# Neighbour sums of steps 2 and 3: one float32 matmul, or two float32r matmuls on a split operand

## The chip, the core and the metric

The kernel runs on one core of one Trainium2 chip. The metric is device microseconds (us) for one execution of the whole program. A core has a matrix engine (TensorE, PE in the profile; its weight loads have a row of their own, PEld), a vector engine (VectorE, DVE), a scalar engine (ScalarE, ACT), GpSimd (POOL), and SyncE (SP), which here only starts transfers. TensorE writes its results to PSUM; the other engines must copy them from there to SBUF before TensorE can use them again as an operand.

## What is computed

There are 128 graphs of 128 nodes with 256 features, and an integer adjacency matrix for each. Layer 0 is a gated graph network of three steps, followed by a residual and a layer norm; layers 1 to 3 are graph attention layers, each with a residual and a layer norm. The part that the change touches is the neighbour sum of layer 0:

```python
A = (adj != 0).astype(x.dtype)
h = x
for i in range(3):
    m = jnp.einsum('bnd,de->bne', h, weight[i])
    aggr = jnp.einsum('bst,bsd->btd', A, m)
    h = _gru_cell(aggr, h, w_ih, w_hh, b_ih, b_hh)
x = _layernorm(x + h)
# then three attention layers with the same adj, e.g.
# Wh = h @ W.T; e = leaky(a1.Wh_i + a2.Wh_j), masked by adj; softmax; h' = att @ Wh
# x = _layernorm(x + h')
```

The kernel sums the neighbours first and multiplies by the weights afterwards (the step's weight and the input weight of the cell are multiplied together once, at the start), so a neighbour sum is a product of h, as it stands, with the 0-or-1 mask A.

## The kernel before

Four graphs make a group (`G = 4`), so the 128 graphs are 32 groups. A group goes through three steps of the gated network (`gru`) and three attention layers (`gat`). All of it is float32.

One step of `gru` does this for a group, for each of the two halves `c` of the 256 features:

1. Line 504: the neighbour sum. For each of the four graphs one matmul takes a 128x128 piece of h (nodes on the partitions) as the stationary operand and the 128x128 mask `am` as the moving operand. The four results fill one PSUM tile called `bank`. Line 506 copies (evicts) it to SBUF, on ScalarE (line 287) or VectorE (line 289), as the planner chooses.
2. Line 421 (`sums`): sums of halves for a Strassen-like scheme, on GpSimd or VectorE.
3. Line 451: the gate matmuls, with 128x128 weights (`whs` for the hidden state, `wcs` for the neighbour sum) and 256 moving columns, and line 456, which adds partial results out of PSUM on VectorE.
4. Lines 530 to 569: the sigmoids (as tanh), the tanh, and the new state, as `hT2`, with features on the partitions.
5. Line 585: the new state is transposed on TensorE back to nodes on the partitions, into a `bank`; line 593 evicts it as `h2`, which is the h of the next step's line 504. After the last step there is no `h2`; the state is added to x instead.

In step 1, h is the input x itself (`xs`), so only the line 504 of steps 2 and 3 uses `h2`. Its matmuls have the names `bank<-am,k` in the profile; those of step 1 have `bank<-am,xs`.

PSUM is split into 5 tiles called `gate` and 3 called `bank`. In SBUF, `k2` names 26 tiles of 512 floats, `k4` 19 of 1024.

The order of work is a plan made when the program is built. `Plan.op` records each piece of work with a cost in ns for every engine that may do it; `Plan.order` runs an event-driven list schedule over these costs, with the older group first, tiles handed out as they come free, and a number of tiles (`own`) kept back for the oldest group. The result fixes the order of the instructions of every engine and, where there is a choice, the engine. Several groups are in work at once, so while one group waits for a vector operation, TensorE works on another group's gates. The costs are only used to plan; on the chip each engine takes its instructions in that order and waits on semaphores.

Of the kernel before, what the change touches and what calls it, by code (L numbers as in the profile page):

```python
# [7 lines left out]

F32 = mybir.dt.float32
I32 = mybir.dt.int32  # L10
AF = mybir.ActivationFunctionType
ALU = mybir.AluOpType
AX = mybir.AxisListType

P = 128
D = 256
KC = D // P
G = 4
# [5 lines left out]
FAR = -5.0 * 2.0 ** 97  # L24
# [174 lines left out]
def adj_resnorm_kernel(  # L199
# [14 lines left out]
    nc = tc.nc  # L214
# [5 lines left out]
    work = ctx.enter_context(tc.tile_pool(name="work", bufs=1))  # L220
# [2 lines left out]

    pools = {"gru": 4, "xs": 2, "adj": 2, "am": 5, "k2": 26, "k4": 19, "fx": 2, "f": 3, "mv": 4, "st": 6, "v": 16,
             "gate": 5, "bank": 3}
    own = ({"k2": 8, "k4": 5, "gate": 2, "v": 5, "fx": 0, "st": 0}, {"k2": 4, "k4": 2, "v": 5, "fx": 0, "st": 0})
    floats = {"gru": 0, "k4": 1024, "xs": 1024, "fx": 256, "f": 8, "mv": 8, "st": 6, "v": 4}
    tags = {t: (n, floats.get(t, 512)) for t, n in pools.items()}
    BOTH = ("DVE", "POOL")
    plan = Plan({t: n for t, (n, _) in tags.items()}, own)  # L230
    slots = {t: [(psum if t in ("gate", "bank") else work).tile([P, w], I32 if t == "adj" else F32, name=f"{t}{i}")
                 for i in range(n)] for t, (n, w) in tags.items() if w}

    def T(b):
        if b.at is None:
            width = 1
            for s in b.shape:
                width *= s
            at = slots[b.tag][b.slot][:, 0:width]
            if len(b.shape) == 2:  # L240
                at = at.rearrange("p (a b) -> p a b", b=b.shape[-1])
            elif len(b.shape) == 3:
                at = at.rearrange("p (a b c) -> p a b c", b=b.shape[-2], c=b.shape[-1])
            b.at = at
        return b.at

    def bank():
        return Buf("bank", GN)

    def here(t):  # L250
        b = Buf(None)
        b.at = t
        return b


    ident = consts.tile([P, P], F32)
    make_identity(nc, ident)
# [3 lines left out]
    A11, A12, N22, S1, S2, S3, S4 = range(7)  # L261
    whs = here(consts.tile([P, 7, 3, P], F32, name="whs"))

    wcs = [here(consts.tile([P, 7, 3, P], F32, name=f"wcs{i}")) for i in range(STEPS)]
    gwT = here(consts.tile([P, 3, KC, D], F32, name="gwT"))
    wa = here(consts.tile([P, 3, 2, D], F32, name="wa"))
    bi = consts.tile([P, 3 * KC], F32, name="bi")
# [17 lines left out]
    def copy(e, dst, src):  # L285
        if e == "ACT":
            nc.scalar.copy(dst, src)  # L287
        else:
            nc.vector.tensor_copy(dst, src)  # L289

    LAND = 1500
    EVICT = {"ACT": 490, "DVE": 600}
    EVICT2 = {"ACT": 370, "DVE": 350}

    def load(dst, src, prio, start=0):

        plan.op({"SP": 450}, lambda e: nc.sync.dma_start(T(dst), src), writes=[dst], prio=prio, lag=LAND, start=start)
# [16 lines left out]
    def hidden_weights(prio):  # L314
        raw = [Buf("k4", 3 * D) for k in range(KC)]
        for k in range(KC):
            load(raw[k], w_hhT[:, k], prio)
        for k in range(KC):

            plan.op({"DVE": 430}, lambda e, k=k: nc.vector.tensor_scalar(  # L320
                T(raw[k])[:, 2 * D:3 * D], T(raw[k])[:, 2 * D:3 * D], 0.5, None, op0=ALU.mult),
                reads=[raw[k]], writes=[raw[k]], prio=prio)
        block_sums(whs, lambda c, k: T(raw[k]).rearrange("p (g c d) -> p g c d", g=3, c=KC)[:, :, c, :], [[r] for r in raw], prio)
# [153 lines left out]
    def gru(g, stage):  # L477

        xs, adj_i, am = Buf("xs", G, D), Buf("adj", G, P), Buf("am", G, P)
        prio = stage(g, 0)  # L480
# [4 lines left out]
                writes=[adj_i], prio=prio)  # L485
        if g == 0:
            input_weights(0, prio)
            hidden_weights(prio)
        plan.op({"DVE": 417}, lambda e: nc.vector.tensor_scalar(T(am), T(adj_i), 0, None, op0=ALU.not_equal),
                reads=[adj_i], writes=[am, turn], prio=prio, port=BOTH)  # L490
        hT = transposed(xs, lambda b, c: T(xs)[:, b, c * P:(c + 1) * P], prio)
        h = None
        for i in range(STEPS):
            prio = stage(g, i)
# [3 lines left out]
            for c in range(KC):  # L498
                b_, a_ = bank(), Buf("k2", GN)

                def fn(e, b_=b_, c=c, h=h):
                    for b in range(G):
                        src = T(xs)[:, b, c * P:(c + 1) * P] if h is None else T(h[c])[:, b, :]
                        nc.tensor.matmul(T(b_)[:, b * P:(b + 1) * P], src, T(am)[:, b, :], start=True, stop=True)  # L504
                plan.op({"PE": 4 * 222}, fn, reads=[am, xs if h is None else h[c]], writes=[b_], prio=prio)
                plan.op(EVICT, lambda e, b_=b_, a_=a_: copy(e, T(a_), T(b_)), reads=[b_], writes=[a_], prio=prio)
                agg.append(a_)
            last = i == STEPS - 1
# [16 lines left out]
            for c in range(KC):  # L525

                o, v, d = rz[c], nn[c], Buf("k2", GN)
# [4 lines left out]
                for gt in range(2):  # L532
                    if c == 0:
                        plan.op({"ACT": 630}, lambda e, gt=gt, o=o, tanh=tanh: tanh(gt, 0, GN, lambda: T(o)[:, gt, :]),
                                reads=[(o, 0), (o, 1)], writes=[(o, 2 + gt)], prio=prio)
                    else:
                        plan.op({"ACT": 365}, lambda e, gt=gt, tanh=tanh, rz=rz: tanh(
                            gt, 0, H, lambda: T(rz[2])[:, gt * H:(gt + 1) * H]),
                            reads=[rz[2]], writes=[(o, 4 + gt)], prio=prio)
                        plan.op({"ACT": 400}, lambda e, gt=gt, o=o, tanh=tanh: tanh(gt, H, GN, lambda: T(o)[:, gt, H:GN]),  # L540
                                reads=[(o, 1), (o, 4 + gt)], writes=[(o, 2 + gt)], prio=prio)
                if c == 1:
                    plan.op({"ACT": 370}, lambda e, v=v, nn=nn: nc.scalar.activation(
                        T(v)[:, 0, 0:H], T(nn[2])[:, 0:H], AF.Identity, bias=bhn[:, 1:2]),
                        reads=[nn[2]], writes=[(v, 0)], prio=prio)
                plan.op({"DVE": 620}, lambda e, o=o, v=v: nc.vector.scalar_tensor_tensor(
                    T(v)[:, 0, :], T(o)[:, 0, :], 1.0, T(v)[:, 0, :], op0=ALU.add, op1=ALU.mult),
                    reads=[(o, 2), (v, 0), (v, 1)], writes=[(v, 2)], prio=prio, port=BOTH)
                if c == 0:
                    plan.op({"DVE": 620}, lambda e, v=v: nc.vector.tensor_add(T(v)[:, 0, :], T(v)[:, 1, :], T(v)[:, 0, :]),  # L550
                            reads=[(v, 2)], writes=[(v, 3)], prio=prio, port=BOTH)
                else:
                    plan.op({"DVE": 350}, lambda e, v=v, nn=nn: nc.vector.tensor_add(
                        T(v)[:, 0, 0:H], T(nn[2])[:, H:GN], T(v)[:, 0, 0:H]),
                        reads=[(v, 2), nn[2]], writes=[(v, 3)], prio=prio)
                    plan.op({"DVE": 350}, lambda e, v=v: nc.vector.tensor_add(  # L556
                        T(v)[:, 0, H:GN], T(v)[:, 1, H:GN], T(v)[:, 0, H:GN]),
                        reads=[(v, 2)], writes=[(v, 4)], prio=prio, port=BOTH)
                plan.op({"ACT": 630}, lambda e, v=v, c=c: nc.scalar.activation(  # L559
                    T(v)[:, 0, :], T(v)[:, 0, :], AF.Tanh, bias=bin_[:, c:c + 1]),  # L560
                    reads=[(v, 3), (v, 4)], writes=[(v, 5)], prio=prio)
# [3 lines left out]
                    reads=[hT[c], (v, 5)], writes=[d], prio=prio, port=BOTH)  # L565
                plan.op({"DVE": 620}, lambda e, d=d, o=o: nc.vector.scalar_tensor_tensor(
                    T(d), T(o)[:, 1, :], 1.0, T(d), op0=ALU.add, op1=ALU.mult),
                    reads=[(o, 3), d], writes=[d], prio=prio, port=BOTH)
                plan.op({"DVE": 620}, lambda e, d=d, v=v: nc.vector.scalar_tensor_tensor(  # L569
                    T(d), T(d), 0.5, T(v)[:, 0, :], op0=ALU.mult, op1=ALU.add),  # L570
                    reads=[d, (v, 5)], writes=[d], prio=prio, port=BOTH)
                hT2.append(d)
            if last:
                y = Buf("k4", G, D)
                plan.op({"SP": 60}, lambda e: nc.sync.dma_start(T(y), x_g), reads=[agg[0]], writes=[y], prio=prio)
                plan.op({"DVE": 417}, lambda e: nc.vector.tensor_scalar(
                    T(am), T(am), 0.0, FAR, op0=ALU.is_equal, op1=ALU.mult), reads=[am], writes=[am], prio=prio, port=BOTH)
            else:
                h2 = [Buf("k2", G, P) for c in range(KC)]
            for c in range(KC):  # L580
                b_ = bank()

                def fn(e, b_=b_, c=c, hT2=hT2):
                    for b in range(G):
                        nc.tensor.transpose(T(b_)[:, b * P:(b + 1) * P], T(hT2[c])[:, b * P:(b + 1) * P], ident)  # L585
                plan.op({"PE": 440}, fn, reads=[hT2[c]], writes=[b_], prio=prio)
                if last:
                    plan.op({"DVE": 620}, lambda e, b_=b_, c=c, y=y: nc.vector.tensor_add(
                        T(y)[:, :, c * P:(c + 1) * P], T(b_).rearrange("p (b d) -> p b d", b=G),
                        T(y)[:, :, c * P:(c + 1) * P]), reads=[b_, turn, (y, 0)],  # L590
                        writes=[(y, b) for b in range(G)], prio=prio)
                else:
                    plan.op(EVICT, lambda e, b_=b_, c=c, h2=h2: copy(
                        e, T(h2[c]), T(b_).rearrange("p (b d) -> p b d", b=G)), reads=[b_], writes=[h2[c]], prio=prio)
            if not last:
                h, hT = h2, hT2
        x1 = Buf("k4", G, D)
# [98 lines left out]
    def stage(g, n):  # L696

        tail = NG - LAST
        return g if g < tail else tail + n, 2 * g + (n >= STEPS)

    for g in range(NG):
        gat(g, *gru(g, stage), stage)
# [47 lines left out]
```

## Time and profile before

| | before |
|---|---|
| time, median of 3 runs (range) | 2700.24 us (2698.6 to 2702.52) |
| span in the profile, granted TensorE clock | 2698.8 us, 0.998 |
| neighbour sums of steps 2 and 3: TensorE instructions | 1024 weight loads and 1024 matmuls (L504, `bank<-am,k`) |
| evictions of `bank` tiles to `k` tiles (all, not only of `h2`) | 456 on ScalarE, mean 583 ns; 228 on VectorE, mean 684 ns |

A page of the profile gives, for each group of equal instructions, the source line, engine and operation, the names of output and inputs, the shape, how many there were, the busy time and the mean duration of one, and then how long the engine stood idle just before them and what ended that. Busy times of TensorE overlap, because matmuls are pipelined; the step from one start to the next says more than the duration. The chain of waits is followed back from the last instruction and says which engine's work set the end.

A float32 matmul of the source stands in the trace as two weight loads and two matmuls; a transpose stands as one of each.

### The profile page before, as it was taken

To read this page: it belongs to the slowest core of one execution; us is meant where nothing else is said; L and a number is where in the kernel's file an instruction comes from. 1 tells how busy PE (TensorE), PEld (TensorE's weight loads), DVE (VectorE), ACT (ScalarE), POOL (GpSimd) and SP (SyncE) were. 2 spreads that over 40 slices of the span, in tenths; PEclk is the share of its full clock that TensorE was granted. 3 is DMA by queue.
4 is the path that set the end of the run, shared out by engine and by line. 5 is a ranking of instruction groups with operands and counts; after the bars stand their busy time and mean duration, and the time that the engine had idled before them with its cause. 6 is when DMAs were issued, how large, how long until landed. Compare 5 with 4: busy or idle time off the path is not lost.

```text
span 2698.8 us, 42460 instructions
## 1 busy us (share of the span) xinstructions
PE 2655.6 (98%) x14536; PEld 2366.9 (88%) x14536; DVE 2019.6 (75%) x6195; ACT 1758.2 (65%) x4633; POOL 603.7 (22%) x749
## 2 busy tenths in 40 slices
PE   8999999999999999999999999999999999999997
PEld 7888889898888888888888888988988988888875
DVE  4676777787777787778777777877778776786796
ACT  4565667666667576666666676666666676765478
POOL 1123222222121221222221221211222211322111
PEclk9999999999999999999999999999999999999999
DMA  3100000000000000001010000000000100000000
GB/s 106 32 13 28 28 13 24 28 29 20 16 21 20 28 28 28 28 1 36 21 36 13 20 24 21 28 28 20 17 28 21 36 21 1 24 9 22 19 1 32
DMA packets 70105, 65.39 MB, mean 24 GB/s; under 512 B 2688, under 2 KB 68224, under 8 KB 69888
## 3 DMA queue, kind: packets, MB, share of 16 engines
q1 hardware_dynamic: 69456, 62.66, 7.7%
q8 instruction: 114, 1.87, 0.3%
q14 instruction: 103, 0.84, 0.1%
q10 hardware_dynamic: 432, 0.01, 0.0%
HBM read 45.89 MB, written 16.78 MB: 23 GB/s over the span
## 4 chain that ended last, share of the span: by engine, by line
PE 90%; DVE 6%; ACT 2%; issue 1%; DMA 0%; POOL 0%; POOLq 0%; ACTq 0%; SPq 0%; DVEq 0%
PE gate L451 61%; PE bank L680 10%; PE bank L504 6%; PE bank L669 6%; PE bank L585 3%; PE bank L620 1%; PE bank L653 1%; DVE fx L611 1%; PE bank L369 1%; PE bank L338 1%; DVE k L686 1%; ACT k L407 1%; DVE k L456 1%; DVE k L289 1%; ACT k L394 0%
## 5 line engine op out<-in xcount | busy, mean ns | idle before, releaser
L451 PE MATMUL gate<-k,whs 128*128 128x256 f32 x4032 | 1201.6, 380 | 3.0 <-DVE k L456 1.4
L451 PE MATMUL gate<-k,wcs 128*128 128x256 f32 x4032 | 1199.2, 379 | 0.0
L451 PEld LDWEIGHTS gate<-k,wcs 128*128 128x128 f32 x4032 | 766.1, 190 | 104.0
L451 PEld LDWEIGHTS gate<-k,whs 128*128 128x128 f32 x4032 | 728.5, 190 | 85.3 <-DVE k L456 2.7
L456 DVE TENSOR_TENSOR k<-gate,k 128x512 f32<-128x512 f32 x576 | 390.4, 686 | 242.3 <-PE gate L451 200.2
L287 ACT COPY k<-bank 128x512 f32<-128x512 f32 (+1 forms) x456 | 262.2, 583 | 207.4 <-PE bank L669 60.9
L680 PE MATMUL bank<-gwT,k 128*128 128x256 f32 x1536 | 350.4, 380 | 3.3 <-ACT k L287 1.5
L680 PEld LDWEIGHTS bank<-gwT,k 128*128 128x128 f32 x1536 | 289.7, 190 | 46.0 <-DVE k L289 4.3
L611 DVE SCALAR_TENSOR_TENSOR fx<-k,wa 128x256 f32<-128x256 f32 x768 | 290.3, 436 | 40.3 <-ACT k L407 38.2
L421 POOL TENSOR_TENSOR k<-k,k 128x256 f32<-128x256 f32 x288 | 236.0, 838 | 372.8 <-DVE k L569 103.6
L394 ACT ACTIVATE k<-k,v 128x256 f32<-128x256 f32 x384 | 190.2, 497 | 185.6 <-DVE v L391 185.1
L407 ACT ACTIVATE k<-k,v,v 128x256 f32<-128x256 f32 x512 | 263.6, 591 | 55.9 <-DVE v L403 53.9
L530 ACT ACTIVATE k<-k,brz 128x512 f32<-128x512 f32 (+1 forms) x384 | 226.9, 620 | 93.2 <-DVE k L456 93.1
L686 DVE SCALAR_TENSOR_TENSOR k<-bank,v,k 128x256 f32<-128x256 f32 x384 | 169.9, 480 | 147.0 <-PE bank L680 145.8
L512 ACT COPY k<-gate 128x512 f32<-128x512 f32 x288 | 164.6, 579 | 127.9 <-PE gate L451 127.0
L564 POOL TENSOR_TENSOR k<-k,k 128x512 f32<-128x512 f32 x82 | 108.5, 1324 | 418.0 <-ACT k L559 418.0
L669 PEld LDWEIGHTS bank<-k,k 128*128 128x128 f32 x1536 | 187.1, 193 | 14.6 <-ACT k L287 5.4
L669 PE MATMUL bank<-k,k 128*128 128x128 f32 x1536 | 189.8, 277 | 8.0 <-DVE k L289 4.0
L289 DVE COPY k<-bank 128x512 f32<-128x512 f32 x228 | 154.3, 684 | 56.2 <-PE bank L504 18.3
L559 ACT ACTIVATE k<-k,bi 128x512 f32<-128x512 f32 x192 | 136.8, 720 | 76.3 <-DVE k L556 59.2
L397 POOL TENSOR_SCALAR v<-v 128x4 f32<-128x4 f32 x96 | 21.1, 220 | 739.3 <-ACT k L394 733.3
L421 POOL TENSOR_TENSOR k<-k 128x256 f32<-128x256 f32 x117 | 100.2, 858 | 340.4 <-DVE k L569 118.2
(78 smaller groups left out, 3166.8 us busy)
## 6 DMA issues: line engine op xcount, KB each, us to landing
xs<-in_x_dram SPq DMA_DIRECT2D x32, 512.0 KB, 3.9
k<-in_x_dram SPq DMA_DIRECT2D x32, 512.0 KB, 3.9
out_dram<-k SPq DMA_DIRECT2D x32, 512.0 KB, 2.9
adj<-in_adj_dram SPq DMA_DIRECT2D x32, 256.0 KB, 2.8
k<-in_gnn_wT_dram SPq DMA_DIRECT2D x3, 256.0 KB, 4.8
k<-in_w_ihT_dram SPq DMA_DIRECT2D x2, 384.0 KB, 5.7
k<-in_w_hhT_dram SPq DMA_DIRECT2D x2, 384.0 KB, 5.7
k<-in_gat_w_dram SPq DMA_DIRECT2D x3, 256.0 KB, 5.1
```

What stands on the lines that cost most here:

```text
L287: nc.scalar.copy(dst, src)
L289: nc.vector.tensor_copy(dst, src)
L394: plan.op({"ACT": 490}, lambda e, b=b: nc.scalar.activation(T(dst)[:, b, :], T(y)[:, b, :], AF.Square, bias=T(mean)[:, b:b + 1], accum_out ...
L407: plan.op({"ACT": 500}, lambda e, b=b: nc.scalar.activation(T(dst)[:, b, :], T(y)[:, b, :], AF.Identity, bias=T(shift)[:, b:b + 1], scale= ...
L421: nc.vector if e == "DVE" else nc.gpsimd).tensor_tensor(T(t)[:, j, :], a(), b(), ALU.subtract),
L451: nc.tensor.matmul(T(dst)[:, j * H:(j + 1) * H], T(w)[:, m, gt, :], moving(m, ms)[1](), start=first and n == 0, stop=n == len(todo) - 1, s ...
L456: plan.op({"DVE": 630}, lambda e: nc.vector.tensor_add(T(o)[:, :, j * H:(j + 1) * H], T(b_).rearrange("p (g n) -> p g n", g=2), T(part).re ...
L530: nc.scalar.activation(T(o)[:, gt, n0:n1], src(), AF.Tanh, bias=brz[:, gt * KC + c:gt * KC + c + 1], scale=0.5)
L611: plan.op({"DVE": 345}, lambda e, b=b, h=h, l=l, f=f, fx=fx, xc=xc: nc.vector.scalar_tensor_tensor(T(fx), T(xc)[:, b, :], 1.0, T(wa)[:, l, ...
L669: nc.tensor.matmul(T(b_)[:, b * P:(b + 1) * P], T(xc)[:, b, c * P:(c + 1) * P], T(pT)[:, b, :], start=True, stop=True)
L680: nc.tensor.matmul(T(b_)[:, (b - b0) * D:(b - b0 + 1) * D], T(aT[k])[:, b * P:(b + 1) * P], T(gwT)[:, l, k, :], start=(k == 0), stop=(k == ...
L686: nc.vector.scalar_tensor_tensor(T(y)[:, b, :], T(b_)[:, (b - b0) * D:(b - b0 + 1) * D], T(rden)[:, b:b + 1], T(xc)[:, b, :], op0=ALU.mult ...
```

## The change

The neighbour sum of steps 2 and 3 is done in float32r, a form of float32 with a shorter mantissa. The mask is 0 or 1 and therefore exact in it. h is split: `hi` is h rounded to float32r as it is evicted, `lo` is the rest, h minus `hi`, also stored as float32r. Two float32r matmuls then add `lo` and `hi` products into the same PSUM tile. The purpose is to replace the two-load, two-matmul float32 product by a form that needs fewer passes through TensorE, at the price of one more vector operation for `lo`.

```diff
-    own = ({"k2": 8, "k4": 5, ...
+    own = ({"k2": 10, "k4": 5, ...
...
+    FRESH = ("k2", "am")
...
+            if b.tag in FRESH:
+                at = work.tile([P, tags[b.tag][1]], F32, tag=f"{b.tag}{b.slot}", name=b.tag)[:, 0:width]
+            else:
+                at = slots[b.tag][b.slot][:, 0:width]
...
+    def R(b):
+        return T(b).bitcast(F32R)
...
-        plan.op({"DVE": 417}, lambda e: nc.vector.tensor_scalar(T(am), T(adj_i), 0, None, op0=ALU.not_equal),
+        plan.op({"DVE": 417}, lambda e: nc.vector.tensor_scalar(R(am), T(adj_i), 0, None, op0=ALU.not_equal),
...
-                        src = T(xs)[:, b, c * P:(c + 1) * P] if h is None else T(h[c])[:, b, :]
-                        nc.tensor.matmul(T(b_)[:, b * P:(b + 1) * P], src, T(am)[:, b, :], start=True, stop=True)
-                plan.op({"PE": 4 * 222}, fn, reads=[am, xs if h is None else h[c]], writes=[b_], prio=prio)
+                        dst = T(b_)[:, b * P:(b + 1) * P]
+                        if h is None:
+                            nc.tensor.matmul(dst, T(xs)[:, b, c * P:(c + 1) * P], T(am)[:, b, :], start=True, stop=True)
+                        else:
+                            for k in (1, 0):
+                                nc.tensor.matmul(dst, R(h[c][k])[:, b, :], R(am)[:, b, :], start=(k == 1), stop=(k == 0))
+                plan.op({"PE": 4 * 222 if h is None else 520}, fn, reads=[am] + ([xs] if h is None else h[c]), writes=[b_], prio=prio)
...
-                h2 = [Buf("k2", G, P) for c in range(KC)]
+                h2 = [[Buf("k2", G, P) for _ in range(2)] for c in range(KC)]
...
-                    plan.op(EVICT, lambda e, b_=b_, c=c, h2=h2: copy(
-                        e, T(h2[c]), T(b_).rearrange("p (b d) -> p b d", b=G)), reads=[b_], writes=[h2[c]], prio=prio)
+                    hi, lo = h2[c]
+                    plan.op(EVICT, lambda e, b_=b_, hi=hi: copy(
+                        e, R(hi), T(b_).rearrange("p (b d) -> p b d", b=G)), reads=[b_], writes=[hi], prio=prio)
+                    plan.op({"DVE": 630}, lambda e, b_=b_, hi=hi, lo=lo: nc.vector.tensor_sub(
+                        R(lo), T(b_).rearrange("p (b d) -> p b d", b=G), T(hi)), reads=[b_, hi], writes=[lo], prio=prio)
```

Beside that, the tiles of the tags `k2` and `am` are allocated anew for each use instead of once, in the same places, and the oldest group keeps 10 instead of 8 `k2` tiles in reserve. The number of tiles stays the same. The order of the whole program is planned again with the new costs.

More of the change, by code (lines that the diff above doesn't have):

```diff
@@ L9 @@
 F32 = mybir.dt.float32
+F32R = mybir.dt.float32r
 I32 = mybir.dt.int32
@@ L225, in adj_resnorm_kernel @@
              "gate": 5, "bank": 3}
-    own = ({"k2": 8, "k4": 5, "gate": 2, "v": 5, "fx": 0, "st": 0}, {"k2": 4, "k4": 2, "v": 5, "fx": 0, "st": 0})
+    own = ({"k2": 10, "k4": 5, "gate": 2, "v": 5, "fx": 0, "st": 0}, {"k2": 4, "k4": 2, "v": 5, "fx": 0, "st": 0})
     floats = {"gru": 0, "k4": 1024, "xs": 1024, "fx": 256, "f": 8, "mv": 8, "st": 6, "v": 4}
@@ L230, in adj_resnorm_kernel @@
     plan = Plan({t: n for t, (n, _) in tags.items()}, own)
+    FRESH = ("k2", "am")
     slots = {t: [(psum if t in ("gate", "bank") else work).tile([P, w], I32 if t == "adj" else F32, name=f"{t}{i}")
-                 for i in range(n)] for t, (n, w) in tags.items() if w}
+                 for i in range(n)] for t, (n, w) in tags.items() if w and t not in FRESH}
     def T(b):
@@ L238, in T @@
                 width *= s
-            at = slots[b.tag][b.slot][:, 0:width]
+            if b.tag in FRESH:
+                at = work.tile([P, tags[b.tag][1]], F32, tag=f"{b.tag}{b.slot}", name=b.tag)[:, 0:width]
+            else:
+                at = slots[b.tag][b.slot][:, 0:width]
             if len(b.shape) == 2:
@@ L576, in gru @@
                 plan.op({"DVE": 417}, lambda e: nc.vector.tensor_scalar(
-                    T(am), T(am), 0.0, FAR, op0=ALU.is_equal, op1=ALU.mult), reads=[am], writes=[am], prio=prio, port=BOTH)
+                    R(am), T(am), 0.0, FAR, op0=ALU.is_equal, op1=ALU.mult), reads=[am], writes=[am], prio=prio, port=BOTH)
             else:
-                h2 = [Buf("k2", G, P) for c in range(KC)]
+                h2 = [[Buf("k2", G, P) for _ in range(2)] for c in range(KC)]
             for c in range(KC):
```

## The prediction

> **What bounds the kernel now.** I first read the page's busy times, then the chain of waits, then the engines by stretch.
>
> ```profile
> PE 2655.6 (98%) x14536; PEld 2366.9 (88%) x14536; DVE 2019.6 (75%) x6195; ACT 1758.2 (65%) x4633; POOL 603.7 (22%) x749
> ...
> PE 90%; DVE 6%; ACT 2%; issue 1%; DMA 0%; POOL 0%; POOLq 0%; ACTq 0%; SPq 0%; DVEq 0%
> PE gate L451 61%; PE bank L680 10%; PE bank L504 6%; PE bank L669 6%; PE bank L585 3%; PE bank L620 1%; PE bank L653 1%; DVE fx L611 1%; PE bank L369 1%; PE bank L338 1%; DVE k L686 1%; ACT k L407 1%; DVE k L456 1%; DVE k L289 1%; ACT k L394 0%
> ```
>
> TensorE is the bound. L504, the neighbour sums of all three steps, is 6% of the chain, about 160 us; steps 2 and 3 are two thirds of it, about 108 us. The stretches show where TensorE is not the bound (columns: stretch, PE, PEld, DVE, ACT, POOL busy, clock, DMA):
>
> ```profile
> 500.00:1000.00 500.00, 499.50 (x2754) 447.00 (x2753) 387.83 (x1173) 329.04 (x873) 122.86 (x150) 1.00 0.08 24
> ...
> 2600.00:2650.00 50.00, 41.93 (x228) 34.04 (x229) 47.91 (x266) 43.39 (x146) 9.31 (x14) 0.97 0.00 1
> 2650.00:2699.00 49.00, 32.09 (x188) 26.82 (x186) 27.03 (x143) 38.16 (x126) 7.20 (x12) 0.94 0.13 44
> ```
>
> In the middle TensorE is full, so a microsecond taken from its queue is a microsecond of the span. Only the last 110 us, where few groups are left, wait for VectorE and ScalarE.
>
> What does one neighbour sum cost TensorE? From the chain of waits around 1006 us (start, length, what):
>
> ```profile
> 1004.83 1.73 PE gate L451 x8
> 1006.56 0.89 PE bank L504 x8
> 1007.45 5.18 PE gate L451 x24
> 1012.63 0.44 PE bank L653 x4
> ```
>
> One L504 operation is eight load-and-matmul pairs in 0.89 us, **111 ns a pair**. A gate pair, with 256 columns, takes 1.73 / 8 = 216 ns. The 128-column transposes of L653 take 110 ns each. The question is whether the 111 ns are the streaming of the columns, which the change shortens, or the weight load, which it may not. The loads have these rows:
>
> ```profile
> L504 PEld LDWEIGHTS bank<-am,k 128*128 128x128 f32 x1024 | 129.7, 192 | 5.6 <-issue 0.5 <-DVE k L686 0.3 <-ACT k L287 0.2
> L585 PEld LDWEIGHTS bank<-ident,k 128*128 128x128 f32 x768 | 92.7, 141 | 21.0 <-ACT k L559 2.7 <-DVE k L569 2.3 <-DVE k L686 1.6
> ```
>
> A load for a float32 matmul takes 192 ns, 51 more than one for a transpose. How long it keeps the next load out is seen where TensorE had stood idle and nothing streams yet. The timeline of the weight loads at two such places, once with one and once with two loads:
>
> ```profile
> 917.99 0.19 PEld L504 LDWEIGHTS bank<-am,k 128*128 128x128 f32 x1 [0.32 <-DVE k L686]
> 917.99 0.30 PEld L504 LDWEIGHTS bank<-am,k 128*128 128x128 f32 x2 [0.32 <-DVE k L686]
> ...
> 680.48 0.14 PEld L585 LDWEIGHTS bank<-ident,k 128*128 128x128 f32 x1 [0.32 <-DVE k L569]
> 680.48 0.20 PEld L585 LDWEIGHTS bank<-ident,k 128*128 128x128 f32 x2 [0.32 <-DVE k L569]
> ```
>
> The second float32 load ends 0.30 - 0.19 = 0.11 us after the first, the second transpose load 0.06 us. So **a float32 load alone occupies about 108 ns**, as long as the pair.
>
> **What the Trainium skill says.** The page "TensorE: Matmul & The Clock Gate", section "LDWEIGHTS (loading the stationary operand)", prices a load at P/1.2 ns for P columns: 107 ns for 128. The float32 loads agree (110 ns in the view above); the transposes' loads are shorter. The same page, "Back-to-back issue gap", prices a matmul at N/2.4 + 2.5 ns, 55.8 ns for one pass of 128 columns. The trace has no such one-pass matmul; its 256-column float32 pair, 216 ns, fits two passes (512/2.4 + 2.5 = 215.8). The section "Weight-path perf modes — Fast Weight Load (FWL) and DoubleRow" says that the fast load is on for 128 weights if the type is not FP32; whether float32r counts as FP32 there it doesn't say, and no trace here shows. "VectorE: DVE Perf Modes", "Why PSUM operands drop a tier", says that float32 from PSUM goes at the base rate; the trace agrees: 686 ns for 512 columns at L456 and 684 at L289, whether one operand or two.
>
> **The change, part by part.**
>
> TensorE. 2 steps x 2 halves x 32 groups = 128 operations, each with 8 float32r matmuls for 4 float32 ones. In the built program a float32r matmul is one load and one matmul, so TensorE has 14,536 of each before and after. What shrinks is the matmul's streaming, from two passes to one. The load is, apart from addresses, the same instruction word as the second load of a float32 matmul. So the new pair is bounded below by one pass, 56 ns, and by the load, 108 to 112 ns; a pair ends with the later one. I take 111 ns, since the load's instruction is unchanged and its row and the idle-start view both give it. 128 x 8 x (111 - 111) = **0 us**. Upper bound: 223 ns, if a float32r matmul streamed as long as a whole float32 one (2 x 111).
>
> VectorE. It gains 128 subtractions of 512 columns with one operand in PSUM; the nearest row is L456, 686 ns: 128 x 0.686 = 87.8 us. In the instruction order of the built programs the planner moves 32 half sums (L421, 0.445 us) and 5 subtractions (L564, 0.737) to GpSimd, and 15 evictions (0.684) to ScalarE: 14.2 + 3.7 + 10.3 = 28.2 us less. Net +60 us: VectorE goes from 2020 to 2080 us, 77%. GpSimd gains 32 x 0.845 + 5 x 1.324 = 34 us, ScalarE 15 x 0.583 = 9 us. In the middle all this lies beside gate matmuls; cost there near nothing. The `hi` eviction, with rounding, I cost like the plain one.
>
> The wait added: the neighbour sum now waits for eviction, then subtraction: about 0.6 + 0.69 + two hand-overs of some 0.2 us (the planner's figures, an assumption), 1.7 us instead of 0.8. Behind the waiting matmul stand all of TensorE's later instructions. But in the built order the TensorE work between the transposes of L585 and the sum that needs them, at the durations above, has a median of 4.8 us (3.0 before), and 95% have at least 3.5 us. The `bank` is held 0.9 us longer, 128 x 0.9 = 115 of 3 x 2700 bank-microseconds; the next matmul group into that bank comes a median of 7.8 us later (6.1 before). So few stalls. TensorE's idle time between 500 and 2500 us was 4.9 us; with VectorE 3% busier I allow half as much again, **+2.5 us**.
>
> The tail. After the last gate matmul the built order has 235 vector instructions instead of 227, some 5.6 us more by the row durations (evictions that used to be on ScalarE). VectorE and ScalarE share the bound there: I take **+3.5 us**. Fresh tiles and the reserve of 10 only move the order.
>
> Sum: 2700 + 0 + 2.5 + 3.5 = **2706 us**.
>
> **Rivals.**
> (1) The float32r load is a fast one, or lets the next load in earlier. Then a pair takes 56 ns, TensorE saves 1024 x 0.055 = 56 us, VectorE at 2080 of 2650 us is still below it: 2700 - 56 + 6 = **2650 us**, faster. For it: the fast-load rule and the 56 ns transposes' loads. Against it: the same instruction word, and that both loads of a float32 pair have 190 to 192 ns in the trace.
> (2) VectorE or the banks become a wait. If every subtraction stood fully in TensorE's way: 128 x 0.69 = 88 us, **2788 us**; a quarter of that is more likely, 2722. For it: VectorE is at 78% in the middle already, and takes its queue in order. Against it: the distances above, and that the plan costs a sum at 520 ns where it takes 890, so TensorE reaches each sum later than planned.
> (3) A float32r matmul of 128 columns streams like a whole float32 one: 1024 x 0.112 = 115 us, **2820 us**. Only the missing trace speaks for it.
>
> **How the numbers follow.** Forecast 0.80 (of it 9% below 2694.6, 35% within 0.2%, 56% above 2705.6, because the tail's order alone can move some us either way), rival 1 0.12, rival 2 0.05, rival 3 0.03. Faster: 0.07 + 0.12 = 0.19; same 0.28; slower 0.45 + 0.08 = 0.53. The forecast holds from about 2692 to 2722; alone that is below 0.8, so the range reaches down to rival 1, 2644 to 2722, and leaves out rivals 2 and 3.
>
> **What would show it.** The loads of the sum still at about 190 ns and eight pairs in 0.89 us on the chain: the load bounds. If eight take 0.45 to 0.55 us, rival 1 is right and the forecast is wrong by its first step. TensorE idle before the sum, ended by VectorE's subtraction, would be rival 2. VectorE near 2080 us, subtraction near 686 ns. The stretch from 2600 us on shows the tail's share.

## The result and the profile after

The changed kernel takes 2713.71 us (2713.59 to 2714.16, 4 runs), the kernel before beside it 2701.38 us: a ratio of 1.0046, 95% interval 1.0029 to 1.0064. It is 12 us slower. The neighbour sums themselves cost the matrix engine the same as before; most of the 12 us is idle time of that engine at other places, and the experiments put it down to the new order of the work. The profile after shows where the time went.

First the busy times and the chain of waits from the page of the changed kernel (lines are 8 to 17 higher in its source: L517 is the neighbour sum of steps 2 and 3, L514 that of step 1, L599 the transposes, L610 the subtraction, L459 the gates, L464 their addition):

```profile
PE 2657.9 (98%) x14536; PEld 2370.1 (87%) x14536; DVE 2064.3 (76%) x6271; ACT 1763.9 (65%) x4648; POOL 620.8 (23%) x786
...
PE 92%; DVE 4%; ACT 1%; issue 1%; DMA 0%; POOL 0%; POOLq 0%; ACTq 0%; SPq 0%; DVEq 0%
PE gate L459 63%; PE bank L697 11%; PE bank L686 6%; PE bank L517 4%; PE bank L599 3%; PE bank L514 2%; PE bank L670 1%; PE bank L637 1%; DVE fx L628 1%; PE bank L377 1%; PE bank L346 1%; DVE k L703 1%; DVE k L559 0%; ACT k L646 0%; DVE k L297 0%
```

The matrix engine has the same 14,536 loads and matmuls and nearly the same busy time (2.3 us more than the 2655.6 us before). L517 and L514 together are 6% of the chain, as L504 was before: nothing was saved there.

Then the groups (line, engine, operation, shape, count, busy us, mean ns):

```profile
L517 PEld LDWEIGHTS bank<-am,k 128*128 128x128 f32 x1024 | 131.6, 193 | 4.8
L610 DVE TENSOR_TENSOR k<-bank,k 128x512 fp32r<-128x512 f32 x128 | 87.0, 684 | 1.9 <-ACT k L295 0.8
L297 DVE CAST k<-bank 128x512 fp32r<-128x512 f32 x53 | 36.1, 683 | 20.7 <-PE bank L599 20.7
```

The load of a float32r operand lasts 193 ns, that of float32 lasted 192. The subtraction costs 684 ns, as its neighbour row said, and rounding to float32r on the way out of PSUM costs what the plain copy cost (684 ns before).

A piece of the chain of waits, where nothing was waited for (start, length, what):

```profile
1010.28 1.73 PE gate L459 x8
1012.00 0.84 PE bank L517 x8
1012.85 1.78 PE gate L459 x8
```

A sum and the eight gate instructions after it take 0.84 + 1.78 = 2.62 us; before they took 0.89 + 1.73 = 2.62 us. The step of 0.05 us only moved from one line to the other. Last, where the matrix engine stood idle, as a list of waits (engine, line, releaser: us in total, times, longest):

```profile
PE gate L459 <- ACT k L532: 9.8, 6, 1.6
PE bank L377 <- DMA xs<-in_x_dram: 7.2, 2, 5.1
PE bank L599 <- DVE k L582: 5.5, 3, 3.4
PE bank L637 <- DVE fx L628: 4.9, 8, 0.7
```

The matrix engine's waits for the same ScalarE line in the kernel before (there L519):

```profile
PE gate L451 <- ACT k L519: 0.8, 1, 0.8
```

One wait of 0.8 us has become six of 1.6 us, one every 330 us: they end at 497.0, 826.7, 1156.5, 1486.2, 1816.0 and 2145.7 us. The planned order has become periodic (in the middle of the program it repeats every four groups; before, it did not), and carries one bad place along. The stretch from 25 to 2550 us, before and then after (stretch, then PE busy):

```profile
25.00:2550.00 2525.00, 2513.89 (x13794) 2249.08 (x13793) 1891.70 (x5638) 1634.17 (x4260) 572.29 (x701) 1.00 0.08 23
```

```profile
25.00:2550.00 2525.00, 2504.96 (x13737) 2241.03 (x13736) 1923.29 (x5675) 1636.44 (x4264) 590.51 (x738) 1.00 0.08 23
```

The engine is idle there for 11.1 us before and 20.0 us after. The last gate matmul with the weights `whs` starts at 2592.3 us before and 2605.4 us after, and in both the program ends 106.5 us later: the whole loss lies ahead of the tail. Of these 13.1 us, 11.0 are idle time between 25 us and that last gate (11.1 before, 22.1 after). The other 2.1 us are longer busy time, and a stretch at half the clock can account for them (PE, PEld, DVE, ACT, POOL busy, then the granted clock):

```profile
129.30:136.10 6.80, 5.77 (x21) 5.02 (x22) 5.77 (x17) 1.19 (x3) 1.96 (x3) 0.50 0.01 2
```

The matrix engine was busy there for 5.8 us at a clock of 0.50, which costs up to 2.9 us; in the profiled execution of the kernel before the clock stayed at 1.00 from 25 us to its last gate. The stretch follows waits of 3.4 and 1.6 us for VectorE (L599 for L582), which end at 127.6 and 130.2 us. Whether these waits lowered the clock was not tried.

What one of the six places looks like is in the chain around 824 us:

```profile
821.35 0.48 DVE fx L628 x3
821.83 0.73 issue
822.57 0.77 DVE fx L628 x5
823.33 0.60 DVE k L577
823.94 0.60 DVE k L559
824.54 0.20 DVE k L642
...
824.78 1.28 ACT k L646 x4
826.06 0.36 ACT k L529
826.42 0.27 ACT k L532
826.69 0.04 issue
826.73 1.99 PE gate L459 x8
```

It is read from below. The eight gate instructions after the wait take 1.99 us instead of 1.73, so a wait costs a little more than its idle time. The gates wait for a PSUM tile that L532 on ScalarE must empty. L529 and L532 stand behind four L646 of another group, which had waited for L642 on VectorE, which stood behind L577, L559 and a run of L628. None of these is a neighbour sum or its subtraction, and the chain shows no wait for a `k2` or `am` tile to come free. Each engine takes its queue in the planned order, so one late vector operation passes through ScalarE's queue to the matrix engine. The 0.73 us of "issue" near the top lies inside one L628 that took 0.94 us instead of 0.42; such an L628 stands ahead of each of the six waits, and the last section comes back to it.

### The profile page after: what moved, and what is told of

The parts are those of the page before. It is cut to its first block, busy times and chain, and to the rows that moved or that the text cites. A ratio compares the mean times of both kernels' runs of the same rounds, so it can differ in the third digit from the quotient of the medians.

```text
span 2711.9 us, 42565 instructions
## 1 busy us (share of the span) xinstructions
PE 2657.9 (98%) x14536; PEld 2370.1 (87%) x14536; DVE 2064.3 (76%) x6271; ACT 1763.9 (65%) x4648; POOL 620.8 (23%) x786
## 4 chain that ended last, share of the span: by engine, by line
PE 92%; DVE 4%; ACT 1%; issue 1%; DMA 0%; POOL 0%; POOLq 0%; ACTq 0%; SPq 0%; DVEq 0%
PE gate L459 63%; PE bank L697 11%; PE bank L686 6%; PE bank L517 4%; PE bank L599 3%; PE bank L514 2%; PE bank L670 1%; PE bank L637 1%; DVE fx L628 1%; PE bank L377 1%; PE bank L346 1%; DVE k L703 1%; DVE k L559 0%; ACT k L646 0%; DVE k L297 0%
## 5 line engine op out<-in xcount | busy, mean ns | idle before, releaser
L459 PE MATMUL gate<-k,whs 128*128 128x256 f32 x4032 | 1207.7, 381 | 11.9 <-ACT k L532 9.8
L459 PE MATMUL gate<-k,wcs 128*128 128x256 f32 x4032 | 1200.3, 379 | 0.0
L459 PEld LDWEIGHTS gate<-k,wcs 128*128 128x128 f32 x4032 | 766.5, 190 | 104.0
L459 PEld LDWEIGHTS gate<-k,whs 128*128 128x128 f32 x4032 | 728.7, 191 | 95.6 <-ACT k L532 13.2
L464 DVE TENSOR_TENSOR k<-gate,k 128x512 f32<-128x512 f32 x576 | 390.1, 684 | 262.0 <-PE gate L459 236.4
L295 ACT COPY k<-bank 128x512 f32<-128x512 f32 (+1 forms) x396 | 227.5, 582 | 183.9 <-PE bank L686 71.6
L429 POOL TENSOR_TENSOR k<-k,k 128x256 f32<-128x256 f32 x318 | 254.3, 815 | 361.7 <-ACT k L295 102.5
L628 DVE SCALAR_TENSOR_TENSOR fx<-k,wa 128x256 f32<-128x256 f32 x768 | 288.5, 434 | 38.3 <-ACT k L415 37.1
L543 ACT ACTIVATE k<-k,brz 128x256 f32<-128x256 f32 (+1 forms) x384 | 224.8, 619 | 41.5 <-DVE k L464 41.5
L429 POOL TENSOR_TENSOR k<-k 128x256 f32<-128x256 f32 x119 | 98.9, 831 | 455.4 <-ACT k L295 184.3
L577 POOL TENSOR_TENSOR k<-k,k 128x512 f32<-128x512 f32 x87 | 111.8, 1291 | 379.5 <-ACT k L572 379.5
L529 ACT ACTIVATE k<-gate,bhn 128x256 f32<-128x256 f32 x288 | 135.2, 470 | 50.4 <-PE gate L459 49.9
```

The source lines that it names most:

```text
L429: nc.vector if e == "DVE" else nc.gpsimd).tensor_tensor(T(t)[:, j, :], a(), b(), ALU.subtract),
L459: nc.tensor.matmul(T(dst)[:, j * H:(j + 1) * H], T(w)[:, m, gt, :], moving(m, ms)[1](), start=first and n == 0, stop=n == len(todo) - 1, s ...
L464: plan.op({"DVE": 630}, lambda e: nc.vector.tensor_add(T(o)[:, :, j * H:(j + 1) * H], T(b_).rearrange("p (g n) -> p g n", g=2), T(part).re ...
L543: nc.scalar.activation(T(o)[:, gt, n0:n1], src(), AF.Tanh, bias=brz[:, gt * KC + c:gt * KC + c + 1], scale=0.5)
L628: plan.op({"DVE": 345}, lambda e, b=b, h=h, l=l, f=f, fx=fx, xc=xc: nc.vector.scalar_tensor_tensor(T(fx), T(xc)[:, b, :], 1.0, T(wa)[:, l, ...
```

## The experiments

Eight kernels were run. The times below are medians beside the kernel before on the same chip, which took 2701.4 us beside the changed kernel, twice the columns, true cost, cost 520 and the first bfloat16 kernel, and 2701.9 us beside the others. "Last gate" is the start of the last gate matmul with `whs`; "idle" is the matrix engine's between 25 and 2550 us (for hi only this takes in 17 us after its last gate).

| kernel | us | ratio to before (95%) | last gate | idle |
|---|---|---|---|---|
| before | 2701.4 | 1 | 2592.3 | 11.1 |
| changed | 2713.7 | 1.0046 (1.0029 to 1.0064) | 2605.4 | 20.0 |
| twice the columns | 2719.9 | 1.0067 (1.0053 to 1.0081) | 2612.1 | 19.9 |
| hi only | 2653.5 | 0.9822 (0.9809 to 0.9836) | 2533.1 | 14.4 |
| true cost | 2740.1 | 1.0142 (1.0129 to 1.0156) | 2623.9 | 28.8 |
| before, cost 520 | 2722.2 | 1.0073 (1.0060 to 1.0085) | 2610.2 | 24.5 |
| same order, no subtraction | 2711.3 | 1.0036 (1.0024 to 1.0049) | 2605.2 | 18.9 |
| before, unplanned work | 2740.5 | 1.0142 (1.0129 to 1.0156) | 2630.5 | 30.4 |
| bfloat16 parts | 2695.3 | 0.9978 (0.9969 to 0.9987) | 2582.4 | 36.1 |
| bfloat16 parts, replanned | 2682.9 | 0.9927 (0.9913 to 0.9941) | 2570.5 | 26.6 |

The idle column explains only a part of each difference. It leaves out the slower start after a wait and the time at half the clock: between 25 us and the last gate of the profiled executions, the clock was 0.5 for 7 us in the changed kernel, for 10 to 20 us in most of the others, for 27 us with the bfloat16 parts, and never in the kernel before.

### Does the load or the streaming bound a float32r pair?

```diff
-   nc.tensor.matmul(dst, R(h[c][k])[:, b, :], R(am)[:, b, :], start=(k == 1), stop=(k == 0))
+   nc.tensor.matmul(T(b_)[:, b // 2 * 2 * P:(b // 2 + 1) * 2 * P], R(h[c][k])[:, b, :],
+                    R(am)[:, b // 2 * 2:b // 2 * 2 + 2, :].rearrange("p a b -> p (a b)"),
+                    start=(k == 1 and b % 2 == 0), stop=(k == 0 and b % 2 == 1))
```

> The changed kernel, with every float32r matmul of the neighbour sum streaming 256 columns (the masks of two graphs) instead of 128 through the same loaded weights. It adds the sums of the two graphs of a pair together, so what is computed is another thing; the time is what counts. If the weight load bounds the pair (about 108 ns[...]), doubling the columns is free: pair 111 to 113 ns, time within 3 us of the changed kernel (2711 to 2718). If the streaming of 128 columns bounds it (two passes, 109 ns), a pair grows to about 216 ns, 1024 x 0.105 = 107 us more, 2820 us.

Measured: 2719.86 us, 6 more than the changed kernel. From its chain of waits:

```profile
1014.06 0.95 PE bank L517 x8
1015.01 1.73 PE gate L459 x8
```

A sum and eight gate instructions take 2.68 us instead of 2.62, so a pair grew by some 7 ns, to about 119 ns, where streaming would have made it 216. 1024 x 0.007 = 7 us, about the difference. Twice the columns are nearly free: the load bounds the pair. The time lies 2 us above the range given, since the pair came out a little longer than expected.

The same from the other side, with half the pairs:

```diff
-   for k in (1, 0):
+   for k in (0,):
...
-   plan.op({"PE": 4 * 222 if h is None else 520}, fn, ...
+   plan.op({"PE": 4 * 222 if h is None else 4 * 112}, fn, ...
...
-   h2 = [[Buf("k2", G, P) for _ in range(2)] for c in range(KC)]
+   h2 = [[Buf("k2", G, P)] for c in range(KC)]
...
-   plan.op({"DVE": 630}, ... nc.vector.tensor_sub(R(lo), ...
```

> The changed kernel with the hi product alone: 4 float32r matmuls per sum instead of 8, no subtraction, no lo tile; h is thus rounded to float32r in these sums. Planned with 448 ns (4 pairs of 112). If a float32r pair costs 111.5 ns because of its weight load, the matrix engine has 128 x 4 x 0.1115 = 57 us less than before; with the same idle time 2643 to 2650 us, and by theory C up to 20 us more than that for idle time of the new order, 2645 to 2670 us.

Measured: 2653.49 us. The last gate matmul comes 59 us earlier than before, where 57 were expected of 512 pairs less; the stretch after it grew from 106.5 to 118.5 us, with a mean clock of 0.87 instead of 0.96, so that 48 us arrive at the end. A float32r product with one part is a gain; with two parts it has as many loads as the float32 matmul had.

### Is the loss the subtraction or the order?

Two theories of the loss stood: (A) the planner was told 520 ns for a sum that takes 890, and so made a bad order; (B) 88 us more on VectorE cost it in any order.

```diff
-   plan.op({"PE": 4 * 222 if h is None else 520}, fn, ...        # the changed kernel
+   plan.op({"PE": 4 * 222 if h is None else 8 * 112}, fn, ...
```

> The changed kernel with one number altered: the planner is told 896 ns (8 pairs of 112 ns) for a neighbour sum of steps 2 and 3 instead of 520. Same instructions, another order. Theory A (the 12 us come from the order that the too low cost produced, with one stall of 2.0 us and one of 0.8 us repeated every 330 us): the repeated stall goes away, 2698 to 2706 us. Rival B (the 88 us of subtractions on the vector engine cost it, in any order): stays at 2711 to 2716 us. The pairs take 111 to 112 ns either way.

Measured: 2740.11 us. Both theories missed. The repeated wait did go away (the gates wait 1.3 us in all for L532), but others came, and the order made with the true cost is 26 us slower still. The opposite edit, in the kernel before:

```diff
-   plan.op({"PE": 4 * 222}, fn, ...                              # the kernel before
+   plan.op({"PE": 4 * 222 if h is None else 520}, fn, ...
```

> The kernel before with one number altered: the planner is told 520 ns instead of 888 for a neighbour sum of steps 2 and 3. No float32r, no subtraction. Theory A (order from a too low cost): slower than before, 2705 to 2715 us, with more idle time of the matrix engine between 25 and 2600 us. Rival B (subtractions): as before, 2698 to 2704 us.

Measured: 2722.21 us. One number that no instruction sees costs 21 us, with the same instructions as before apart from the engine chosen for some of them. So order alone can cost more than the change did, and more than A had forecast; B is not needed to explain the loss, though this run does not exclude it. But A in its form, that the false number is what harms, fell with the run before. What is left is theory (C): the order decides, and a new one is not better for being made from truer costs. The next run keeps the order of the changed kernel and takes out the suspected work:

```diff
-   plan.op({"DVE": 630}, lambda e, b_=b_, hi=hi, lo=lo: nc.vector.tensor_sub(R(lo), T(b_)..., T(hi)), reads=...
+   plan.op({"DVE": 630}, lambda e: None, reads=...
...
-   nc.tensor.matmul(dst, R(h[c][k])[:, b, :], ...
+   nc.tensor.matmul(dst, R(h[c][0])[:, b, :], ...
```

> The changed kernel with its own planned order, but the 128 subtractions are not issued; both float32r matmuls of a pair read hi, so hi counts twice and lo is left out of what is computed. Matrix engine work and the order of all else stay. Theory B (the 88 us of subtractions on the vector engine cost the 12 us): 2698 to 2704 us. Theory C (the order of the queues decides where the matrix engine stands idle; the subtractions were planned for and lie beside it): 2707 to 2716 us, with the same two stalls repeated every 330 us.

Measured: 2711.27 us, 2.4 below the changed kernel (9.4 above the kernel before beside it, where the changed kernel was 12.3 above), with overlapping intervals of the ratios. VectorE's busy time fell by 70 us, from 2064.3 to 1993.8 us. The matrix engine's largest waits in this run:

```profile
PE gate L459 <- ACT k L532: 9.8, 6, 1.6
PE bank L377 <- DMA xs<-in_x_dram: 8.0, 2, 4.9
PE bank L636 <- DVE fx L627: 4.9, 8, 0.7
PE bank L599 <- DVE k L582: 3.9, 2, 3.4
```

Six waits for L532, 9.8 us, the longest 1.6, and eight of L636 for L627, 4.9 us: the same as with the subtractions, to the tenth of a microsecond (L636 and L627 are L637 and L628 above). Theory B falls for this order: the planned subtractions lie beside the gates and cost some 2 to 3 us, as forecast. One rival is left in the 9.4 us: the fresh allocation of the `k2` and `am` tiles is part of every form of the changed kernel and was not tried alone; only the chain above speaks against it. The counter-test keeps the order of before and adds as much vector work that no plan knows of, behind each eviction of a sum:

```diff
+   def out_(e, b_=b_, a_=a_, h=h):
+       copy(e, T(a_), T(b_))
+       if h is not None:
+           nc.vector.tensor_copy(slots["fx"][0].bitcast(mybir.dt.bfloat16), T(b_))
-   plan.op(EVICT, lambda e, b_=b_, a_=a_: copy(e, T(a_), T(b_)), reads=[b_], writes=[a_], prio=prio)
+   plan.op(EVICT, out_, reads=[b_], writes=[a_], prio=prio)
```

> The kernel before in its own planned order, with 128 more vector operations that the plan does not know of: the result of each neighbour sum of steps 2 and 3 is read once more out of PSUM into a scratch tile (128 x about 0.6 us = 77 us of the vector queue). Nothing else waits for it. Theory B (such work costs about 12 us): 2710 to 2716 us. Theory C (a fixed order stands little unplanned work, since the vector queue falls behind the places that the plan gave it): clearly more than 12 us, 2720 to 2745 us. If the vector engine had real slack beside the matrix engine: 2700 to 2704 us.

Measured: 2740.52 us. The added operations in its groups, and where its matrix engine waits:

```profile
L509 DVE CAST fx<-bank 128x512 bf16<-128x512 f32 x128 | 87.8, 686 | 27.5 <-ACT k L287 26.9
```

```profile
PE gate L451 <- DVE k L456: 11.1, 13, 2.4
PE bank L589 <- DVE k L573: 7.6, 7, 2.9
```

88 us of vector work cost 39 us where the plan had no place for it, although VectorE is busy for 76% of the span. Some of this is waiting rather than work: the added operations stood 27 us for ScalarE, and VectorE's queue with them. That they hold their bank longer matters little: the matrix engine waited for L509 0.2 us before matmuls and 0.7 us before loads. Theory C stands: about the same amount of work cost 2 to 3 us in a plan that knew of it and 39 us at a place in the queue that no plan had chosen.

### A type whose load is short

The remaining question was whether 8 short pairs would pay if the loads were faster. The same split with bfloat16 parts, and a bfloat16 copy of the mask:

```diff
+   ab = Buf("ab", G, P // 2)
+   plan.op({"DVE": 417}, lambda e: nc.vector.tensor_copy(T(ab).bitcast(BF16), T(am)), reads=[am], writes=[ab], ...
...
-   nc.tensor.matmul(dst, R(h[c][k])[:, b, :], R(am)[:, b, :], ...
+   nc.tensor.matmul(dst, half(h[c], k)[:, b, :], T(ab).bitcast(BF16)[:, b, :], ...
```

> The same split with bfloat16 parts: hi is h rounded to bfloat16, lo the rest rounded to bfloat16, a bfloat16 copy of the mask; 8 matmuls per sum as in the changed kernel. It keeps 16 bits of h instead of 24 in these sums. Other differences: both parts lie in one k2 tile, 24 instead of 26 k2 tiles, 8 in reserve, one more mask copy per group on the vector engine (32 x about 0.4 = 13 us). If the weight load of float32 size bounds the pair and a 16-bit load is the fast one: pair 56 to 81 ns, 1024 x 0.031 to 0.055 = 31 to 56 us less on the matrix engine, so 2655 to 2685 us. If the pair is bound by something else, for example a fixed cost of each load and matmul: pair stays near 110 ns, 2708 to 2720 us.

Measured: 2695.33 us. The loads in the groups, and two sums on the chain:

```profile
L523 PEld LDWEIGHTS <-k 128*128 128x128 bf16 x1024 | 66.1, 98 | 11.6 <-DVE k L615 0.3
```

```profile
1001.53 0.89 PE bank L523 x16
```

A load lasts 98 ns instead of 193, and a pair takes 0.89 / 16 = 56 ns. That is the price of one isolated pass of 128 columns in the Trainium skill, "TensorE: Matmul & The Clock Gate", section "Back-to-back issue gap" (55.8 ns); for a stream of loads and matmuls the same section gives about 81 ns, the upper end of the range above, and the measured 56 ns decide. The section "Weight-path perf modes — Fast Weight Load (FWL) and DoubleRow" says that the fast load is on for 128 weights of a type other than FP32; the bfloat16 load agrees with 98 ns, and the float32r load, 193 ns, behaves like the FP32 load of 192. The matrix engine has 1024 x 0.055 = 56 us less to do, yet only 6 us arrived, and the time lies outside both ranges given. The idle time grew from 11.1 to 36.1 us in the middle alone, and for 27 us the clock was at half; by themselves these do not add up to the whole. By theory C another order should give some of it back:

```diff
-   MARGIN = 500
+   MARGIN = 800
...
-   plan.op({"PE": 4 * 222 if h is None else 520}, fn, ...
+   plan.op({"PE": 4 * 222 if h is None else 450}, fn, ...
```

> The kernel with the bfloat16 parts (16 bits of h in these sums), planned otherwise: 450 ns per sum, which is what its 8 pairs took (8 x 56), instead of 520, and a margin of 800 instead of 500 ns that the planner leaves between a result of another engine and its use on the matrix engine. Theory C (the 53 us that its matrix engine saves went into idle time of the order): less idle time, 2670 to 2688 us. If the idle time comes from the vector engine's load whatever the order: as the first such kernel, 2690 to 2698 us.

Measured: 2682.85 us, the idle time down to 26.6 us. With 16 bits of h in two of three sums this beats the kernel before by 19 us and the changed kernel by 31. The two edits were made together; which of them helped isn't separated. The hi-only kernel is faster, but leaves `lo` out altogether.

## Why the prediction held, step by step

**The matrix engine, 0 us: right.** The argument was the load, read from two loads after an idle stretch and from the unchanged instruction. Load 193 ns, sum with gates 2.62 us in both kernels, pair 119 ns with twice the columns and 56 ns with a short load confirm the argument. Rival 1 (a fast load) and rival 3 (slow streaming) are both excluded by these rows.

**VectorE, +60 us: too high, and of no consequence.** 128 subtractions took 87.0 us against 87.8, but the busy time rose only by 2064.3 - 2019.6 = 44.7 us. Their durations are not what they add: records on VectorE overlap (the vector operations of the chain above follow each other in 0.60 us, with records of 0.68), and taking the subtractions out of the same order freed 70.5 us, 0.55 each. Less the 28 us forecast to move away, that is 42 us, close to the 44.7. That the subtractions cost nearly nothing in the middle was right: without them, in the same order, 2 to 3 us are gained.

**The stall term, +2.5 us: mis-sized.** This is the term that failed. The last gate matmul starts 13.1 us later, with 11.0 us more of idle time. I had scaled the idle time by VectorE's load; the runs put it down to the order, which has six copies of one bad place. Even nearly the same instructions lose 21 us by an order made from another number (2722.2 us). The clock, at half for 6.8 us, was no term of the sum at all. The distance between the transposes and the sum, on which the term leaned, was indeed long enough: the loads and matmuls of L517 waited for nothing in the trace. The stalls came at other instructions, which the prediction had not considered.

**The tail, +3.5 us: wrong.** 106.5 us both times; the vector instructions added after the last gate did not lengthen it.

**Rival 2 (VectorE or the banks become a wait, 2722 to 2788 us)** named the right kind of loss, idle time ahead of the matrix engine, and the wrong cause: the subtractions are not it, nor do the banks that they hold show among the matrix engine's larger waits. Sum of the terms: 0 + 13 + 0 = 13 us, against 6 forecast.

**Luck.** That the time came out slower, and within the 2692 to 2722 us of the forecast, owes something to luck. Of the two terms that made it slower, the tail was nothing and the stalls had another cause, and a new order moved other kernels by 21 and 26 us, more than the 16 us from 2706 us to the upper end.

What stays open is why one planned order has a stall that another lacks. Ahead of each of the six waits, with and without the subtractions, one L628 took 0.94 instead of 0.42 us while a GpSimd operation (L429) ran. That makes VectorE's queue 0.5 us late, less than the wait of 1.6 us; whether the wait would go without it was not tried.

## What to carry to other kernels

Before trading one matmul for two cheaper ones, count loads: here a pair cost about the longer of its load and its streaming, and a type that shortened only the streaming saved nothing at 128 columns. When an engine is full and the order is planned ahead, any edit buys a new order, and a new order with nearly the same work was worth 21 and 26 us here; measure a change beside the same instructions in another order before putting a small difference down to its work. Give new work to the plan, too: planned, 88 us of it cost 2 to 3 us, unplanned 39.

## What was not expected of the hardware

- A float32r matmul with 128x128 weights takes about 112 ns for 128 columns and about 119 ns for 256; its load lasts 193 ns, as for float32, and 98 ns for bfloat16.
- Rounding to float32r or bfloat16 while emptying PSUM costs the same as a plain copy: 683 and 686 ns for 512 columns on VectorE, where the copy takes 684.
- A vector operation with two operands in SBUF (L628) took 0.94 us instead of 0.42 where it met a GpSimd operation that ran from 821.51 to 822.35 us. In the changed kernel 22 of the 768 L628 took over 0.6 us, and all 22 overlapped a GpSimd operation; 35 others overlapped one by more than 0.1 us and were not slowed so. The kernel before has 23 slow ones too (its L611), so these meetings alone are not what the two kernels differ in. The timeline of the changed kernel on VectorE and on GpSimd:

```profile
821.69 0.94 DVE L628 SCALAR_TENSOR_TENSOR fx<-k,wa 128x256 f32<-128x256 f32 x1
```

```profile
821.51 0.84 POOL L429 TENSOR_TENSOR k<-k 128x256 f32<-128x256 f32 x1 [3.81 <-DVE k L297]
```
